# Where the combining of a band is traced: directly behind its deformable products instead of two slots later

## The chip, the cores and the metric

The kernel runs on one core of a Trainium2 chip. The metric is the device time of one execution in microseconds (us). Engines by the names of the profile: PE (TensorE: matrix products and transposes; PEld is its weight load), DVE (VectorE), ACT (ScalarE), POOL (GpSimd), and SP (SyncE, which here only issues DMAs). Each engine works through its own list of instructions in order.

## The reference

Two layers on 32 images of 96 channels and 56 x 56 pixels, float32.

Layer 0 is an inverted bottleneck: 1x1 convolution to 576 channels, normalisation and SiLU; a 3x3 depthwise convolution, normalisation and SiLU; a squeeze-and-excite gate; a 1x1 convolution back to 96 channels; the input is added.

Layer 1 is the part that the change touches (`sampled` are nine bilinear samples per pixel at learned offsets):

```python
y = x * ca * sa                                   # channel and spatial attention, from spectra
aux = concat([y, coord, freq_e], 1)
offset = conv3x3(aux, off_w)                      # 18 channels: 9 taps x 2
gate = sigmoid(conv1x1(relu(conv3x3(aux, dg1_w)), dg2_w))
y_base = conv3x3(y, base_w)
sampled = grid_sample_taps(y, xx + off[:, :, 0], yy + off[:, :, 1])
y_def = einsum('bcthw,oct->bohw', sampled, def_w) + def_b
z = (1 - gate) * y_base + gate * y_def
zn = (z - mean(z)) / sqrt(var(z) + 1e-5) * bn_g + bn_b    # over all images
return relu(zn + x)
```

## The kernel before

**Tiling.** Layer 1 goes through each image in 7 bands of 8 rows (224 bands in all, index `n`), and each band in two halves (h = 0, 1) of 7 blocks each 4 pixels wide. In this text half-band number 2n+h is called "half 2n+h". The samples of a block are a matrix product: `weights` multiplies two loaded tables `wc` and `wr` into sampling weights (one DVE instruction per half, L709; "product k" is the one for half k), `sample_tiles` multiplies transposed image blocks by them (PE, L738) and ACT copies the samples into a tile `v` (L742). `pack` (L749, ACT) moves the last two taps of `v` into free partitions. `deform` (L757, PE) then multiplies `v` by the deformable weights into the PSUM bank `pd`; both halves of a band write into the same bank, and there is one such bank. `combine` reads `pd` and forms z with three DVE instructions (L796, L797, L798) and its statistics with a fourth (L799). `store` writes z to memory (L1060, issued by POOL). After the last band of an image, L1067 joins the statistics.

**What runs beside it.** `layers` interleaves three Python generators into one stream of traced instructions. Beside the bands of image b run layer 0 and the attention of image b+1 (`attend`: L329, L396, L420, L379 and small products; L373 on POOL) and the hidden part of layer 0 of image b+2 (`hidden`: L169 on PE, L173 on ACT, nine taps on DVE, L260 and L262). `pump` advances these by one "slot" and runs what has been put into `later` with a slot number. `find` does the offsets of band n+2: joint convolution (L615), copy of the offsets (L664), a maximum (L675), base convolution (L644).

**The order around the change.** In each half the loop does: `prepare` (table loads by SP, L702 and L703); `sample_tiles` for the first 3 blocks; three slots; then, once per half, the `ends` of the half before (`end_half`: `deform`, and, after h = 1, `join`, which calls `combine`); then `block_channels` (L720 on POOL, transposes L724 on PE) where due; then `weights` for the next half; then `sample_tiles` for the other 4 blocks with four slots, and `pack`. So the deformable products of band n's second half are traced inside half 2n+2, and the next instruction that `weights` traces there is product 2n+3.

Rows of the next image arrive in the padded tile `yp` by SP (L594) with an attention factor by POOL (L596), and DVE multiplies them (L602).

**Who sets the final order.** Tile's scheduler reorders the traced instructions of each engine by priority (trace order) and by its own estimate of when inputs are ready, and it sets the semaphores. SP is excluded (`manual_schedule`): its order is the traced one. One instruction is pinned by hand:

```python
def weights(nc, p, wc, wr):
    p["tc"].keep_in_program_order(nc.vector.tensor_tensor(wc, wc, wr, ALU.mult))
    return wc
```

`keep_in_program_order` adds an edge without a semaphore: the instruction stays behind the one that was traced just before it on the same engine. It says nothing of later ones, and nothing of two pinned instructions among themselves unless other edges join them.

Of the kernel before, what the change touches and what calls it, by code (L numbers as in the profile page):

```python
# [751 lines left out]
def deform(nc, p, pd, v, h):  # L752

    out = pd[:C, :BW].rearrange("c (q w) -> c q w", q=RB)[:, :, h * W // 2 : (h + 1) * W // 2]
    for k in range(KA):
        ks = slice(0, 128 if k else C)
        nc.tensor.matmul(out.rearrange("c q (t x) -> c t q x", x=TS), p["w"]["def"][ks, k],  # L757
                         v[ks, k].rearrange("c t s (r x) -> c t (s r) x", r=TS),
                         start=(k == 0), stop=(k == KA - 1))
# [33 lines left out]
def combine(nc, p, j, pd, yb, gate, st):  # L793

    z = p["q2"].tile([C, BW], FP, name="z")
    nc.vector.scalar_tensor_tensor(z, pd[:C, :BW], p["w"]["cv"]("def_b"), yb, ALU.add, ALU.subtract)  # L796
    nc.vector.scalar_tensor_tensor(z, gate, 1.0, z, ALU.add, ALU.mult)  # L797
    nc.vector.scalar_tensor_tensor(z, z, 0.5, yb, ALU.mult, ALU.add)  # L798
    nc.vector.bn_stats(st[:, j], z)  # L799
    return z  # L800
# [152 lines left out]
def layers(tc, a, dp, x1d, zd, stats, far):  # L953
# [8 lines left out]
    with ExitStack() as ctx:  # L962
# [26 lines left out]
        streams, later = [], []  # L989
        slot = 0  # L990
# [68 lines left out]
        def store(b, j, z):  # L1059
            nc.gpsimd.dma_start(zd[b][:, j * BW : (j + 1) * BW], z)  # L1060

        def join(n, pd, gate, st):
            b, j = bands[n]
            z = combine(nc, p, j, pd, ybs[n], gate, st)
            later.append((slot + 7, lambda: store(b, j, z)))
            if j == NBD - 1:
                nc.vector.bn_aggr(stats[:, b], st)  # L1067

        def end_half(n, h, v, gate, st):
            if h == 0:  # L1070
                pds[n] = p["pd"].tile([128, 512], FP, name="pd")
            deform(nc, p, pds[n], v, h)
            if h:
                pd = pds.pop(n)
                later.append((slot + 2, lambda: join(n, pd, gate, st)))

        ends, pds = [], {}

# [41 lines left out]
        for n, (b, j) in enumerate(bands):  # L1120
            if j == 0:
                st = p["st"].tile([C, NBD, 6], FP, name="st")
# [7 lines left out]
            for h in range(2):  # L1130
                v = p["vp"].tile([128, NTAP, NTH, 2, TP], FP, name="v")
                prepare(2 * n + h + READY + AHEAD)
                s = ready.pop(0)
                yt = yts.pop(0)
                for i, group in enumerate(GROUPS):
                    sample_tiles(nc, p, yt, s, v, group)
                    for _ in range(group[0][0], group[-1][1]):
                        next(more, None)
                        pump()
                    if i == 0:  # L1140
                        for end in ends:
                            end()
                        ends.clear()
                        if h == 1 and n + 1 < len(bands):
                            yts.append(block_channels(nc, p, yp, bands[n + 1][1], 0))
                        ready.extend(weights(nc, p, *ws) for ws in loads[:1])
                        del loads[:1]
                        if h == 0:
                            yts.append(block_channels(nc, p, yp, j, 1))
                pack(nc, v)  # L1150
                if h == 0:
                    if n % 2 == 0:
                        gates.extend(gates_of(nc, p, hids[n // 2]))
                    gate = gates.pop(0)
                ends.append(lambda n=n, h=h, v=v, gate=gate, st=st: end_half(n, h, v, gate, st))
# [360 lines left out]
```

## Time and profile before

| | us |
|---|---|
| median of 3 runs | 9004.03 (8993.15 to 9010.88) |
| profiled execution | 8993.57, its span 8991.8 |
| PE busy | 8180.0 (91%) |
| DVE busy | 7174.8 (80%) |
| ACT busy | 5380.8 (60%) |
| POOL busy | 2600.4 (29%) |
| mean granted clock of TensorE | 0.94 |
| of this: one steady stretch, 4000 to 5000 | PE 953.68, DVE 842.19, ACT 622.27, POOL 318.64 |

The bands take the span from about 430 to 8705; the last 290 us are the normalisation. An image takes some 263 us. Images come in two forms that alternate, because the streams beside the bands don't divide evenly into slots; so a place in the order is the same again two images later. How to read it: "A <- B" in a list of waits is idle time of the engine of A, ended by B, as total, times, longest. In a timeline, "x3" merges three instructions of a line, and a bracket holds the idle time before the first of them and what ended it. A matmul instruction of the program on float32 shows as two records, a transpose as one.

### The profile page before, as it was taken

Reading aid. Unit: us, or ns where it says so; the run is one execution under the profiler, and the core shown is the slowest. Engines: PE = TensorE matmul, PEld = TensorE weight load, DVE = VectorE, ACT = ScalarE, POOL = GpSimd, SP = SyncE. Lnnn points to the kernel's source line nnn. Section 1 sums busy time; section 2 is a strip of 40 time slices with the busy share of each in tenths; the row PEclk is TensorE's granted clock in tenths of the full one; section 3 lists DMA queues with packets and bytes.
Section 4 is the critical chain, followed back from the end, with each engine's and each line's share of the span. In section 5 each row is a group of like instructions: output and inputs, shape, how many; then the busy total and the mean of one; then the engine's idle time right before and its main releaser. Section 6 shows DMA issues by size and latency. Waiting matters only on the chain. (4 is left out here: it accounts for less than half of the span.)

```text
span 8991.8 us, 137403 instructions
## 1 busy us (share of the span) xinstructions
PE 8180.0 (91%) x52406; PEld 5185.1 (58%) x52406; DVE 7174.8 (80%) x6821; ACT 5380.8 (60%) x10486; POOL 2600.4 (29%) x2608
## 2 busy tenths in 40 slices
PE   5899999999999999999999999999999999999960
PEld 3456565666656656665666666566566656666640
DVE  7688888888888888888888888888888888887333
ACT  2356666666666666666666666666666666666553
POOL 0133233333323332332332333233333323332210
PEclk9889999999999999999999999999999999999985
DMA  2356666666666666666666666666666666666669
GB/s 80 109 144 167 164 167 164 164 155 155 169 167 167 169 163 150 159 164 167 169 167 160 153 159 166 168 167 168 164 151 162 166 166 168 168 165 146 130 189 417
DMA packets 1068756, 1486.47 MB, mean 165 GB/s; under 512 B 590190, under 2 KB 839838, under 8 KB 1055806
## 3 DMA queue, kind: packets, MB, share of 16 engines
q1 hardware_dynamic: 858995, 985.20, 46.7%
q10 hardware_dynamic: 153803, 329.80, 10.2%
q0 software_dynamic: 55296, 162.60, 6.7%
q8 instruction: 420, 6.88, 0.4%
q14 instruction: 242, 1.98, 0.1%
HBM read 1064.29 MB, written 412.65 MB: 164 GB/s over the span
## 5 line engine op out<-in xcount | busy, mean ns | idle before, releaser
L262 DVE SCALAR_TENSOR_TENSOR acch<-hp,w,acch 128x1512 f32<-128x1512 f32 (+1 forms) x2250 | 4348.3, 1933 | 38.3
L615 PE MATMUL mm<-yp,c_jointW 104*128 104x448 f32 x4032 | 1655.9, 562 | 1.0 <-DMA yp<-fqd 1.0
L720 POOL COPY ybl<-yp 96x448 f32<-96x448 f32 x896 | 1035.1, 1183 | 1541.2 <-PE mm L724 1541.0
L757 PE MATMUL pd<-v,c_def 128*96 128x224 f32 (+1 forms) x6272 | 1429.6, 375 | 53.8 <-DVE z L796 29.0
L757 PEld LDWEIGHTS pd<-v,c_def 128*96 128x96 f32 (+1 forms) x6272 | 1039.5, 173 | 349.1 <-issue 74.5
L615 PEld LDWEIGHTS mm<-yp,c_jointW 104*128 104x128 f32 x4032 | 768.0, 194 | 758.2 <-issue 724.7
L738 PE MATMUL mm<-wc,yt 64*96 64x144 f32 x12544 | 1086.6, 302 | 115.7 <-ACT yb L649 44.8
L738 PEld LDWEIGHTS mm<-wc,yt 64*96 64x96 f32 x12544 | 845.6, 165 | 430.2 <-issue 193.2
L173 ACT ACTIVATE hp<-mm,sh,inv 128x392 f32<-128x392 f32 (+2 forms) x1216 | 812.0, 672 | 461.9 <-PE mm L169 416.4
L169 PE MATMUL mm<-xt,w 96*128 96x392 f32 (+3 forms) x2688 | 1056.8, 527 | 34.4 <-DMA xt<-in_x 33.4
L742 ACT COPY v<-mm 96x288 f32<-96x288 f32 (+1 forms) x2688 | 1003.6, 442 | 126.9 <-PE mm L738 81.4
L329 PE MATMUL mm<-hq,w3s 128*96 128x392 f32 x2048 | 796.8, 536 | 99.2 <-DMA hq<-h2d 92.4
L709 DVE TENSOR_TENSOR wc<-wc,wr 128x1008 f32<-128x1008 f32 x448 | 562.7, 1256 | 365.8 <-DMA wr<-hd 338.6
L644 PE MATMUL mm<-yp,c_base0W 96*64 96x224 f32 x8064 | 827.3, 357 | 0.0
L668 POOL DMA_DIRECT2D od<-at x224 | 185.6, 829 | 2217.9 <-DVE at L664 1515.6
L749 ACT COPY v<-v 32x448 f32<-32x448 f32 x1344 | 755.2, 562 | 29.7
L644 PEld LDWEIGHTS mm<-yp,c_base0W 96*64 96x64 f32 x8064 | 554.0, 135 | 275.4 <-issue 61.5
L726 ACT COPY yt<-mm 128x384 f32<-128x384 f32 (+1 forms) x896 | 350.5, 439 | 544.3 <-PE mm L724 543.8
L635 ACT ACTIVATE hid<-mm,c_dg1b 50x448 f32<-50x448 f32 x224 | 140.6, 628 | 862.9 <-PE mm L615 853.6
L329 PEld LDWEIGHTS mm<-hq,w3s 128*96 128x96 f32 x2048 | 339.1, 174 | 453.1 <-issue 311.0
L222 ACT ACTIVATE acch<-acch,sh,inv 128x1568 f32<-128x1568 f32 x288 | 488.3, 1695 | 180.3 <-DVE acch L262 167.0
L476 POOL TENSOR_TENSOR o<-o,xc 96x392 f32<-96x392 f32 x256 | 374.3, 1462 | 738.9 <-ACT o L339 737.3
(194 smaller groups left out, 9146.8 us busy)
## 6 DMA issues: line engine op xcount, KB each, us to landing
h2d<-acch ACTq DMA_DIRECT2D x288, 784.0 KB
wc<-hd SPq DMA_DIRECT2D x896, 252.0 KB
wr<-hd SPq DMA_DIRECT2D x448, 504.0 KB
hq<-h2d SPq DMA_DIRECT2D x128, 980.0 KB
hq<-h2d SPq DMA_DIRECT2D x128, 784.0 KB
hq<-x1d SPq DMA_DIRECT2D x768, 98.0 KB
ht<-od SPq DMA_DIRECT2D x224, 252.0 KB
hd<-ho ACTq DMA_DIRECT2D x224, 252.0 KB
```

Source lines behind the costliest of these rows:

```text
L169: nc.tensor.matmul(pt[p0 : p0 + w1.shape[1], : rows * W], w1, xts[hf][:, r0 * W : (r0 + rows) * W], start=True, stop=True)
L173: nc.scalar.activation(h1[lo:hi, row0 : row0 + rows, 1 : 1 + W], pt[lo:hi, : rows * W].rearrange("p (h w) -> p h w", h=rows), AF.Silu, bia ...
L262: nc.vector.scalar_tensor_tensor(acc[:, lo:hi], win, wk, acc[:, lo:hi], ALU.mult, ALU.add)
L329: nc.tensor.matmul(pts[half][:C, :EW], w3s[:, ch], hq, start=(i == 0), stop=False)
L615: nc.tensor.matmul(view, weights[:, k], yp[:channels, r0 : r0 + RB, dx + PD - 1 : dx + PD - 1 + W], start=(k == 0), stop=(k == NTAP - 1))
L644: nc.tensor.matmul(pb[i * BC : (i + 1) * BC, : BW // 2].rearrange("p (h w) -> p h w", h=RB // 2), w["base"][:, k], yp[:C, r0 + i * RB // 2 ...
L709: p["tc"].keep_in_program_order(nc.vector.tensor_tensor(wc, wc, wr, ALU.mult))
L720: nc.gpsimd.tensor_copy(yb[:, :, s], blocks)
L738: nc.tensor.matmul(pt[k][:C, (t - lo) * KP : (t - lo + 1) * KP], yt[ps, t], s[ps, t * KP : (t + 1) * KP], start=True, stop=True)
L742: nc.scalar.copy(v[:C, :, lo:hi, k].rearrange("c k t p -> c t k p"), pt[k][:C, : (hi - lo) * KP].rearrange("c (t k p) -> c t k p", t=hi - ...
L749: nc.scalar.copy(v[C:, 1 + 2 * i : 3 + 2 * i], v[i * QC : (i + 1) * QC, KA:])
L757: nc.tensor.matmul(out.rearrange("c q (t x) -> c t q x", x=TS), p["w"]["def"][ks, k], v[ks, k].rearrange("c t s (r x) -> c t (s r) x", r=T ...
```

## The change

`combine` is traced inside `end_half`, directly behind the deformable products of h = 1, instead of by `pump` two slots later. That puts it ahead of `block_channels`, of `weights` and of the second `sample_tiles` of the half, where before it came in the middle of the latter's slots. `store` is still put into `later` for 7 slots after the combining, so it comes two slots earlier as well. Nothing else changes: the instructions, their shapes and the pools are the same.

```diff
@@ def end_half(n, h, v, gate, st)
             deform(nc, p, pds[n], v, h)
             if h:
                 pd = pds.pop(n)
-                later.append((slot + 2, lambda: join(n, pd, gate, st)))
+                join(n, pd, gate, st)
```

## Prediction

> **What bounds the kernel now.** I read the page first, then busy time by stretches, the waits by engine, and the timeline of two stretches. Engine row of the page:
>
> ```profile
> PE 8180.0 (91%) x52406; PEld 5185.1 (58%) x52406; DVE 7174.8 (80%) x6821; ACT 5380.8 (60%) x10486; POOL 2600.4 (29%) x2608
> ```
>
> Stretches (us; busy of each engine; granted clock; DMA share; GB/s), two of them short ones around a wait of TensorE:
>
> ```profile
> 4000.00:5000.00 1000.00, 953.68 (x6125) 604.43 (x6123) 842.19 (x758) 622.27 (x1219) 318.64 (x315) 0.96 0.66 165
> ...
> 3628.40:3635.25 6.85, 4.88 (x8) 2.33 (x9) 5.99 (x3) 3.27 (x5) 4.31 (x4) 0.50 1.07 296
> ```
>
> TensorE (PE) works 954 us of each 1000, VectorE (DVE) 842. So a delay on DVE costs only where it makes PE wait. PE's list of waits says which DVE work does that today:
>
> ```profile
> PE mm L329 <- DMA hq<-h2d: 92.4, 30, 4.1
> ...
> PE pd L757 <- DVE z L796: 29.0, 25, 3.0
> ...
> PE mm L738 <- DVE wc L709: 4.6, 1, 4.6
> ```
>
> The combining holds PE 25 times (29.0 us, and 20.4 us more on PE's weight loads): the one `pd` bank isn't free yet. The weights product L709 holds it once. That is the term to watch, because the change moves L709.
>
> **What the change moves.** Six lines of trace order, no instruction more or less. `weights` (L709) is pinned: it may not pass the DVE instruction traced just before it. Before, in the half-bands with h=0 that instruction is some convolution or reduction. After, it is the last of the combining, L799 (L1067 in the last band of an image). In the built order of the changed kernel all 223 products of odd number stand behind the previous band's L799; before, 2 did. And L709 of the following even half, pinned to an older instruction, is no longer held behind it: in 67 places the pair is swapped, product 2n+2 ahead of 2n+1, two bands per image in images 1 to 30 and seven in the last image. SP's queue keeps its order to the instruction; POOL's differs by one store per image (L1060 ahead of L668); on ACT 268 of 10647 instructions are out of the old order, on PE 1121 of 27771: mainly deform products (L757) set ahead of the sampling L738 that now waits.
>
> So the wait added is L738's, for a product that comes late. Queued behind L738 on PE is everything: PE takes its matmuls in order. Queued ahead of L709 on DVE are L796 to L799 and what is dealt between them.
>
> **(a) Fourth band of each image.** Half 175, DVE and then PE, timeline before (start, us, line, idle before in brackets):
>
> ```profile
> 3756.03 0.69 DVE L664 COPY at<-mm 18x224 f32<-18x224 f32 x2
> 3756.65 1.44 DVE L709 TENSOR_TENSOR wc<-wc,wr 128x1008 f32<-128x1008 f32 x1
> 3758.01 0.60 DVE L675 TENSOR_REDUCE top<-at 18x1 f32<-18x448 f32 x1
> 3758.54 7.42 DVE L262 SCALAR_TENSOR_TENSOR acch<-hp,w,acch 128x1568 f32<-128x1568 f32 x3
> 3765.99 0.68 DVE L796 SCALAR_TENSOR_TENSOR z<-pd,c_cvec,yb 96x448 f32<-96x448 f32 x1
> 3766.59 1.96 DVE L262 SCALAR_TENSOR_TENSOR acch<-hp,w,acch 128x1512 f32<-128x1512 f32 x1
> ...
> 3773.62 0.61 DVE L799 BATCH_NORM_STATS2 st<-z 96x6 f32<-96x448 f32 x1
> 3776.81 0.68 DVE L602 SCALAR_TENSOR_TENSOR yp<-yp,ca,sab 96x448 f32<-96x448 f32 x1 [2.58 <-DMA yp<-x1d]
> ```
>
> ```profile
> 3764.87 1.05 PE L396 MATMUL mm<-c_FU,hq 112*128 112x116 f32 x8
> 3765.84 0.98 PE L738 MATMUL mm<-wc,yt 64*96 64x144 f32 x12
> ```
>
> Product 175 is done at 3758.1 and PE wants it at 3765.84: 7.8 us of slack. In the changed order DVE does L664, L675, four L262, L796, product 176, L797, L262, L798, then L602, L799 and only then product 175. L602 is the point: it reads rows whose DMA landed at 3776.81, and that landing hangs on the GpSimd and SP queues (GpSimd busy from 3752.44 to 3768.8 before it issued the offsets; SP issued the rows at 3772.01, behind the read of those offsets), which the change leaves alone. So 3776.81 + 0.68 + 0.61 (L799) + 1.19 (product) = 3779.3. PE arrives at 3765.84 with six deform instructions put ahead (12 of the 14 records that took 2.81: 2.4 us), themselves held until L796 frees `pd` at 3756.72 + 0.60 + 7.42 + 1.96 + 0.68 = 3767.4. PE therefore loses 3779.3 - 3765.84 - 2.4 = 11.1 us. Images come in two alternating forms; in the other one (half 161) L602 started at 3515.41, the product ends at 3517.9, L738 was due at 3502.87 and only two deform instructions (0.8 us) stand ahead: 14.2. Mean 12.7 us per image.
>
> **(b) First band of each image** (behind the last band's combining). Half 169: product 170 waits for its load until 3652.12 as before and ends at 3653.8; then two L262 (4.2), L796, L797, L798 (1.9), L379 (0.9), L799 and L1067 (1.0), product 169 (1.2): 3663.0. PE was due at 3658.23, one deform instruction now stands ahead (0.4 in half of the cases): 4.7 lost. In the other form (half 155) L379 could start only at 3400.18, when its rows had landed; 0.92 + 0.62 + 0.34 + 1.19 more give 3403.3, against 3393.94 and 0.4: 8.9, less the 1.4 that PE waited for `pd` right behind it and no longer does: 7.5. Mean 6.1.
>
> **(c) The five other odd halves of an image.** In three the delay (6.4 to 7.6 us) is within the slack (10.5 to 14.1) or nearly so (4.9 of 6.4). In two, halves 173 and 177, the product ends 4.5 and 5.5 us after L738's old start, but 1.9 to 3.5 us of other matmuls now stand ahead, and PE arrives later after (b) and (a) while DVE does not. I take 0; bounds 0 and 4 us.
>
> **(d) Clock.** When PE waited 3.52 us for `hq` (to 3630.36), the clock stood at 0.50 from 3628.40 to 3635.25, and the next eight L329 records took 5.26 us; the eight before took 2.87. A wait of 1.98 us at 3705.44 drew 6.8 us of half clock too. Two new waits per image at 2.4 each: 4.8. [...]
>
> **(e) What goes.** With PE this much later, the hidden rows that it waits for today (92.4 us in 30 waits, 3.1 per image) have landed, and their half clock (2.4) goes too: -5.5. Between -1 (they slip along with PE) and -9 (bank waits for ACT, 44.8 and 43.6 us in all, go as well).
>
> **(f) At nothing.** The earlier store of z (POOL is busy 29%) and the later release of `wr`: half 177's load, issued at 3774.41, slips to 3779.3, but its product isn't due before some 3805. Freeing `pd` earlier: 49.4 us of PE's waits is the most it can return; (b) has counted its part, and (a) adds one such wait, so 0.
>
> **Sum.** 12.7 + 6.1 + 4.8 - 5.5 = 18.1 us per image; 30 images: 543. The last image, with seven swapped pairs and DVE only 30% busy: four halves (433 to 439) end 11.5, 10.9, 9.2 and 5.6 us late, less 1.5 each for deform work put ahead: about 31. In all 574. The profiled execution took 8993.6 us (span 8991.8), 10.5 below the median of 9004.03: 8993.6 + 574 = 9568, say 9565.
>
> **Rivals.**
> 1. *The slack holds, about 9050.* DVE idles 15%; if it runs so far ahead that combining and product are done in time, only (a)'s landing stays, at part of its price: 30 x 2 us. Against: the slack of 7.8 us is measured with DVE as it is, and in (a) DVE has to wait for a landing, not for itself. 6 in 100.
> 2. *Faster, about 8950.* The only mechanism is `pd`: combining at once frees it, and the 49.4 us go. It decides only if product 2n+1 isn't late by more than about 1.5 us per image; seven products per image would each have to keep their slack. 3 in 100.
> 3. *It feeds back, about 9900.* DVE stands in front of L796 while PE is late, the convolutions behind it (L260, L262) stop, and so do hidden rows and ACT; then (e) is 0, (c) 4 and each image loses another 3 to 5 us: 30 x 28 + 31 = 871, 9865. For it: DVE at 84%. Against: the period grows by 7%, which gives DVE 18 us more per image. 13 in 100.
>
> **Numbers.** Forecast 78 in 100: 30 x (half of (a)+(b)) = 280 with nothing else gives about 9275 at its low end; all bounds at their dear end, 30 x 26.6 + 31, gives 9820. The range 9250 to 9820 leaves out rival 1 and 2 and part of 3. A change under 0.2% (18 us) can't be told from none: faster 0.03, same 0.03, slower 0.94.
>
> **What would show it.** Right: PE's waits list L738 <- L709 with about 60 waits near 10 us, 450 to 650 us together; granted clock below 0.94 in the mean; the wait for `hq` short. Wrong: if that row stays under 100 us, (a) and (b) are wrong, most likely by L602's landing being earlier. If PE's waits for ACT or `hq` grow, rival 3.

## The result, and the profile after

The changed kernel takes 9729.35 us (median of 4 runs, 9706.02 to 9749.40) against 8999.76 for the kernel before (8993.15 to 9010.88): a ratio of 1.081 (95% interval 1.078 to 1.084). It is slower by some 730 us; 565 were forecast. The profiled execution took 9721.11 us, its span 9719.3, which is 727.5 longer than before. Engine row of the page after:

```profile
PE 8441.1 (87%) x52406; PEld 5350.3 (55%) x52406; DVE 7176.6 (74%) x6821; ACT 5415.7 (56%) x10486; POOL 2704.7 (28%) x2608
```

The counts are those of before, and DVE is as busy as before (7176.6 against 7174.8). PE's part of the span splits the loss in two: 261 us more busy time for the same matmuls, and 9719.3 - 8441.1 = 1278 us idle where 812 stood, so 466 us more idle. Waits of PE after:

```profile
PE mm L738 <- issue: 479.1, 91, 11.3
PE mm L329 <- DMA hq<-h2d: 87.8, 27, 5.4
...
PE pd L757 <- DVE z L796: 49.7, 17, 8.4
```

The first row is new. The profile calls its releaser "issue": the wait for the product sits on PE's sequencer, ahead of the matmul (in half 175 a semaphore wait of 9.97 us of PE's weight-load queue, which ends at 4043.6, where the product's first L738 starts). Taken half by half, the first L738 of the halves concerned starts 0.10 us after the end of its own product L709 (median), so the releaser is L709. The same holds for 29 waits that the list puts under PE's own L757 (23.9 us) and 7 under ACT's L771 (34.3 us). Idle time of PE in front of such an L738 is 545 us in all, in 131 waits; 9.7 before. By half (halves 28 to 425, mean per image): first band's second half 4.9 us, third band's 0.9, fourth band's 9.3, fifth band's 2.0, the other three 0.

The fourth band of the image that was shown for before; DVE, then PE (start, length, line; idle before in brackets):

```profile
4030.26 0.68 DVE L796 SCALAR_TENSOR_TENSOR z<-pd,c_cvec,yb 96x448 f32<-96x448 f32 x1
4030.86 1.43 DVE L709 TENSOR_TENSOR wc<-wc,wr 128x1008 f32<-128x1008 f32 x1
...
4034.82 0.97 DVE L798 SCALAR_TENSOR_TENSOR z<-z,yb 96x448 f32<-96x448 f32 x1
4041.18 0.68 DVE L602 SCALAR_TENSOR_TENSOR yp<-yp,ca,sab 96x448 f32<-96x448 f32 x1 [5.39 <-DMA yp<-x1d]
4041.78 0.62 DVE L799 BATCH_NORM_STATS2 st<-z 96x6 f32<-96x448 f32 x1
4042.32 1.19 DVE L709 TENSOR_TENSOR wc<-wc,wr 128x1008 f32<-128x1008 f32 x1
```

```profile
4031.72 2.49 PE L757 MATMUL pd<-v,c_def 96*96 96x224 f32 x12
4043.61 1.85 PE L738 MATMUL mm<-wc,yt 64*96 64x144 f32 x12 [9.40 <-issue]
4045.39 1.67 PE L169 MATMUL mm<-xt,w 96*128 96x392 f32 x2
```

(This is half 175 again; it has moved from 3766 to 4044.) The first L709 is product 176, the second product 175: the pair is swapped, and product 175 stands behind the landing that L602 waits for. PE idles 9.40 us. Behind the wait the twelve L738 records take 1.85 us; before they took 0.98, at a granted clock of 1.00. Stretches around it (busy of PE, PEld, DVE, ACT, POOL; granted clock; DMA share; GB/s):

```profile
4034.00:4037.73 3.73, 0.21 (x2) 0.00 (x0) 1.78 (x2) 0.00 (x0) 2.67 (x3) 1.00 0.26 21
4037.73:4051.40 13.67, 7.79 (x39) 6.40 (x41) 6.44 (x7) 3.04 (x6) 1.68 (x4) 0.50 0.63 155
4051.40:4055.00 3.60, 3.60 (x34) 2.95 (x36) 3.56 (x2) 3.19 (x8) 1.97 (x1) 1.00 0.01 2
```

Half clock lasts 13.67 us, of which PE worked 7.79. Over the whole span, the long last stretch of the normalisation left out, PE works 1159 us at half clock, 685 before. The twelve L738 records take about twice their time at half clock (1.85 us against 0.98). If all of the work at half clock does, half of the 474 us difference, 237 us, is an estimate of what the clock adds: nearly all of the 261 us of busy time.

### The profile page after: what moved, and what is told of

It reads as the page before. It is cut to its first block, busy times and chain, and to the rows that moved or that the text cites. A ratio compares the mean times of both kernels' runs of the same rounds, so it can differ in the third digit from the quotient of the medians.

```text
span 9719.3 us, 137423 instructions
## 1 busy us (share of the span) xinstructions
PE 8441.1 (87%) x52406; PEld 5350.3 (55%) x52406; DVE 7176.6 (74%) x6821; ACT 5415.7 (56%) x10486; POOL 2704.7 (28%) x2608
## 3 DMA queue, kind: packets, MB, share of 16 engines
q1 hardware_dynamic: 858995, 985.20, 43.6%
## 5 line engine op out<-in xcount | busy, mean ns | idle before, releaser
L720 POOL COPY ybl<-yp 96x448 f32<-96x448 f32 x896 | 1152.9, 1314 | 2457.4 <-PE mm L724 2456.9
L615 PE MATMUL mm<-yp,c_jointW 104*128 104x448 f32 x4032 | 1702.2, 574 | 1.0 <-DMA yp<-fqd 1.0
L738 PE MATMUL mm<-wc,yt 64*96 64x144 f32 x12544 | 1179.3, 316 | 549.6 <-issue 479.1
L757 PE MATMUL pd<-v,c_def 128*96 128x224 f32 (+1 forms) x6272 | 1462.7, 381 | 96.4 <-DVE z L796 49.7
L738 PEld LDWEIGHTS mm<-wc,yt 64*96 64x96 f32 x12544 | 912.5, 174 | 853.6 <-issue 692.6
L757 PEld LDWEIGHTS pd<-v,c_def 128*96 128x96 f32 (+1 forms) x6272 | 1055.9, 176 | 419.0 <-issue 103.6
L615 PEld LDWEIGHTS mm<-yp,c_jointW 104*128 104x128 f32 x4032 | 788.9, 199 | 782.4 <-issue 747.1
L169 PE MATMUL mm<-xt,w 96*128 96x392 f32 (+3 forms) x2688 | 1118.6, 551 | 34.7 <-DMA xt<-in_x 33.6
L329 PE MATMUL mm<-hq,w3s 128*96 128x392 f32 x2048 | 774.6, 524 | 101.7 <-DMA hq<-h2d 87.8
L709 DVE TENSOR_TENSOR wc<-wc,wr 128x1008 f32<-128x1008 f32 x448 | 554.0, 1237 | 348.7 <-DMA wr<-hd 338.5
L260 DVE TENSOR_SCALAR acch<-hp,w 128x1568 f32<-128x1568 f32 x270 | 282.6, 1047 | 469.1 <-ACT hp L173 452.4
```

Source lines behind the costliest of these rows:

```text
L169: nc.tensor.matmul(pt[p0 : p0 + w1.shape[1], : rows * W], w1, xts[hf][:, r0 * W : (r0 + rows) * W], start=True, stop=True)
L329: nc.tensor.matmul(pts[half][:C, :EW], w3s[:, ch], hq, start=(i == 0), stop=False)
L615: nc.tensor.matmul(view, weights[:, k], yp[:channels, r0 : r0 + RB, dx + PD - 1 : dx + PD - 1 + W], start=(k == 0), stop=(k == NTAP - 1))
L720: nc.gpsimd.tensor_copy(yb[:, :, s], blocks)
L738: nc.tensor.matmul(pt[k][:C, (t - lo) * KP : (t - lo + 1) * KP], yt[ps, t], s[ps, t * KP : (t + 1) * KP], start=True, stop=True)
```

## The experiments

Theory: the time goes where a product (L709) that is pinned behind the combining holds PE's sampling, and into the half clock behind those waits. Rival: the early combining itself is dear, because it holds VectorE up in front of L796. Each kernel was compared with the kernel before on the same chip; the first four shared one set of its runs (median 9007.3), the next four another (9009.5), the last two a third (8995.8). In the diffs the changed kernel is the old side unless it is said otherwise.

### 1. The product traced first

```diff
                     if i == 0:
+                        ready.extend(weights(nc, p, *ws) for ws in loads[:1])
+                        del loads[:1]
                         for end in ends:
                             end()
 ...
-                        ready.extend(weights(nc, p, *ws) for ws in loads[:1])
-                        del loads[:1]
```

> The changed kernel, but weights is traced ahead of the ends, so the product of an odd half is pinned to the same instruction as before the change and not behind the combining; the combining stays directly behind its deformable products. Theory (the late product is the whole cost): about 9000 us, waits of TensorE at L738 near 0, granted clock 0.94; perhaps 8950 if freeing the pd bank sooner is worth its 49 us. Rival (the early combining itself costs, by holding VectorE in front of L796 while TensorE is late): 9400 or more, with VectorE's waits at L796 near the 448 us of the changed kernel.

9019.98 us, ratio 1.0015 (1.0003 to 1.0026). The combining is still directly behind its products, but 2 of 223 odd products stand behind it instead of all. Waits of DVE for `pd` and of PE for DVE's release of it in this kernel, and after them DVE's row of the changed kernel:

```profile
DVE z L796 <- PE pd L757: 215.3, 93, 12.0
...
PE pd L757 <- DVE z L796: 56.4, 30, 6.2
```

```profile
DVE acch L260 <- ACT hp L173: 452.4, 102, 10.6
DVE z L796 <- PE pd L757: 447.9, 96, 11.8
```

The rival falls: with the combining as early as in the changed kernel, DVE waits 215 us for `pd` (188 before), not 448, and the loss is gone. DVE's long waits in the changed kernel belong to the late product, not to the early combining. The gain from freeing `pd` earlier, up to 49 us, didn't come either: PE waits 56 us for it.

### 2. The pin taken away

```diff
-    p["tc"].keep_in_program_order(nc.vector.tensor_tensor(wc, wc, wr, ALU.mult))
+    nc.vector.tensor_tensor(wc, wc, wr, ALU.mult)
```

> The changed kernel with the pin on L709 taken away, nothing else. Theory: the scheduler puts the products ahead of the combining again, the cost of the change goes, and what is left is the worth of the pin itself: 9000 to 9150 us. Rival (early combining costs): stays above 9400.

9254.77 us, ratio 1.028 (1.026 to 1.030): two thirds of the loss go, and the expected upper end, 9150, is passed. PE's waits for products are down to 11.6 us. What is left comes with another order: products now float ahead to where their tables haven't landed, and DVE stands before them.

```profile
DVE wc L709 <- DMA wr<-hd: 706.7, 213, 15.6
```

It was 338.6 us in 120 waits before. Some of that reaches PE: its waits for DVE's small product L563 are 81.1 us, 4.4 before. That this is all of the 247 us that are left is not shown. With the combining traced early the pin is worth having (9020 us in number 1, 9255 without it); what counts is the instruction it is tied to.

### 3. One slot instead of two

```diff
 # against the kernel before
-                later.append((slot + 2, lambda: join(n, pd, gate, st)))
+                later.append((slot + 1, lambda: join(n, pd, gate, st)))
```

> The kernel before with the combining one slot after its deformable products instead of two; weights is still traced ahead of it. Theory: within 0.3% of the kernel before (8975 to 9025), since no product is pinned behind the combining. Rival (a dose of early combining costs a dose of time): about half of the change's loss, 9350.

8902.56 us, ratio 0.988 (0.986 to 0.990): faster than both kernels, which neither theory expected. There is no dose of loss in an earlier combining. The gain is PE busy time (8100.0 us against 8180.0) with the idle time as before (817 against 812). In the kernel before, PE waits twice per image for PSUM banks that ACT still reads, in the stretch behind half 176:

```profile
PE mm L738 <- ACT yb L649: 44.8, 29, 1.9
PE mm L738 <- ACT hp L173: 43.6, 31, 1.9
```

With one slot the first row is gone and the second is

```profile
PE mm L738 <- ACT hp L173: 5.8, 11, 1.7
```

and the half clock in their place, 10.0 us per image, is 0.4 (table below). That the waits draw this half clock is argued from the place; no run takes the waits alone away. The idle time itself came back at other places (L724 on POOL's copies, 37.2 us; L615 on the frequency rows, 34.4 us).

### 4. L602 kept out of the product's way

```diff
-    nc.vector.scalar_tensor_tensor(rows, rows, p["ca", b], sab, ALU.mult, ALU.mult)
+    p["tc"].keep_in_program_order(nc.vector.scalar_tensor_tensor(rows, rows, p["ca", b], sab, ALU.mult, ALU.mult))
```

> The changed kernel with L602 pinned behind the instruction traced before it, which takes it out from between L798 and L799 in the fourth band of an image. Theory (a): product 175 no longer waits for the landing of the rows and ends about 5.4 us sooner, so the wait of 9.3 us per image there falls to about 4, 160 us less in all and up to 60 us of clock: 9500 to 9600 us. Rival (the place of L602 is of no account, the product is late by VectorE's own work): 9700 to 9740.

9495.82 us, ratio 1.055 (1.051 to 1.058): just below the expected range, and some 235 us less than the changed kernel, by the medians as by the ratios. The wait in the fourth band is 4.8 us instead of 9.3, waits for products are 389 us in all instead of 545. In profiled executions 9719.3 - 9477.0 = 242 us less, 75 of them busy time of PE (8365.9). The landing of the rows was half of the wait in (a).

### 5 to 7. The change in some bands alone

```diff
-                join(n, pd, gate, st)
+                if bands[n][1] == 2:              # 6: == NBD - 1;  7: not in (2, NBD - 1)
+                    join(n, pd, gate, st)
+                else:
+                    later.append((slot + 2, lambda: join(n, pd, gate, st)))
```

> Of the change, only the combining of the third band of each image is traced directly behind its deformable products (so the late product is that of the fourth band's second half, step (a)); the six others keep their two slots. Theory: 31 waits of about 9.3 us and 3 to 4 us of half clock behind each, 9350 to 9500 us. Rival (the 9.3 us there are a consequence of what other bands do): under 9200.

> Only the combining of the last band of each image is traced directly behind its products (step (b)). Theory: 31 waits of about 4.9 us and 2 to 3 us of clock each, 9180 to 9320 us. Rival: under 9100.

> The change in all bands but the third and the last of each image (step (c), taken as 0 because TensorE would be late already). If the three parts add up, this is what the two others leave of the 727 us: 50 to 150 us, 9050 to 9150. If the parts of (c) were only covered by the lateness from (a) and (b), it is more: two waits of 2 us and their clock in each image, 9150 to 9260. If (c) is 0 by itself: 8990 to 9040.

| kernel | us | ratio to before (95%) | span over before | PE busy over before | PE idle over before | waits for products |
|---|---|---|---|---|---|---|
| changed, all bands | 9729.35 | 1.081 (1.078-1.084) | +727.5 | +261.1 | +466.4 | 545 |
| 5: third band alone | 9255.52 | 1.028 (1.025-1.032) | +244.6 | -22.7 | +267.3 | 308 |
| 6: last band alone | 9203.11 | 1.022 (1.020-1.025) | +212.2 | +80.9 | +131.3 | 161 |
| 7: the five others | 9236.43 | 1.026 (1.021-1.031) | +210.8 | +147.5 | +63.3 | 82 |

(Spans, busy and idle from each profiled execution, against 8991.8, 8180.0 and 811.8. Numbers 5 to 7 have two executions each; the two of number 7 are 64 us apart, and the profiled one is the shorter.) The first row of PE's waits for products in numbers 5, 6 and 7:

```profile
PE mm L738 <- issue: 300.2, 33, 11.2
```

```profile
PE mm L738 <- issue: 125.7, 26, 8.6
```

```profile
PE mm L738 <- issue: 49.8, 25, 4.6
```

The three spans add up to 668 of 727.5, so the parts are nearly independent, and each costs about as much as the others. But they pay in different coin. The long waits of number 5 cost idle time and no busy time in the sum. Number 7, with short waits of 0.9 and 1.1 us per image in the third and fifth band, has 147 us more busy time. That is neither what step (c) nor what step (d) of the prediction said, and number 5 stayed below its expected range, which had added a clock cost to each wait. Number 6 lies in its range. Number 7 lies in its second range, but not for the reason given there: its waits, 2.0 us per image, aren't longer than the 2.9 of the changed kernel, so the lateness from (a) and (b) had covered nothing.

Where the half clock lies, worked out from the clock's record: us of half clock per image, mean over 28 images, by the half-band (counted from 0 within the image) in which it began:

| half | before | changed | 5 | 6 | 7 | one slot (3) |
|---|---|---|---|---|---|---|
| 0 | 0 | 10.7 | 0 | 10.1 | 0 | 0 |
| 1 | 2.4 | 0.1 | 3.2 | 0.5 | 2.7 | 3.5 |
| 3 | 3.7 | 3.9 | 3.2 | 3.9 | 4.0 | 4.4 |
| 5 | 0.2 | 6.3 | 0 | 0.1 | 10.2 | 0.4 |
| 6 | 0 | 12.9 | 13.4 | 0 | 0 | 0 |
| 8 | 10.0 | 3.2 | 0 | 10.4 | 5.7 | 0.4 |
| others | 5.5 | 6.4 | 5.9 | 5.2 | 4.8 | 6.7 |
| sum | 21.8 | 43.5 | 25.7 | 30.1 | 27.4 | 15.4 |

Number 5 trades the 10.0 us of half 8 for 13.4 in half 6. Of these 13.4 PE is idle for 6.4, with no matmul to slow down; of the 10.0 before it was idle for 1.5. Number 6 adds 10.1 in half 0 and keeps most of the rest. Number 7 adds 10.2 in half 5, as 15 stretches of some 20 us in 28 images.

### 8. The combining last in its step

```diff
-                join(n, pd, gate, st)
+                joins.append(lambda: join(n, pd, gate, st))
 ...
                         if h == 0:
                             yts.append(block_channels(nc, p, yp, j, 1))
+                        while joins:
+                            joins.pop(0)()
 ...
```

> The combining traced in the same step as its deformable products, but behind block_channels and weights. Theory: no product is pinned behind it, so none of the change's loss: 8900 to 9020, between the kernel with one slot (8903) and the one with weights first (9020). Rival (any combining ahead of the next slot costs): over 9100.

9006.31 us, ratio 0.9998 (0.9985 to 1.0011), as expected. Together with number 1 it brackets the cause. In both the combining is early, and `weights` is traced ahead of it, so no product is tied to it; both take the time of the kernel before. The changed kernel, with `weights` behind the combining in the same step of the loop, takes 8% more.

### 9 and 10. Three slots, and the best kernel with L602 pinned

```diff
 # 9, against the kernel before
-                later.append((slot + 2, lambda: join(n, pd, gate, st)))
+                later.append((slot + 3, lambda: join(n, pd, gate, st)))
 # 10: the diff of 3 and that of 4 together
```

> The kernel before with the combining three slots after its deformable products instead of two. Theory of a slack that is wide on this side too (no product is pinned behind it, the pd bank is wanted again only in the next half): 8990 to 9060 us. If the gain of one slot (-1.2%) is a trend, the mirror of it: about 9100.

> One slot instead of two, and L602 pinned as in the run before that pinned it. If the rows' landing holds VectorE up in the best kernel too, some 20 to 60 us less than its 8903; if its gain of one slot is a matter of the clock alone, 8880 to 8960.

Number 9: 8931.39 us, 0.993 (0.992 to 0.995), below both of its expectations. Number 10: 8959.88, 0.996 (0.995 to 0.997). So one slot isn't a step of a trend: three are faster than two as well, with the same thing missing (half 8 has 0.2 us of half clock, 10.0 with two slots). Two slots happen to give an order in which PE runs into ACT's banks there. Why the scheduler deals it so, was not tried. Pinning L602 doesn't help the best kernel (57 us slower by medians, 68 by the ratios), though it helped the changed one: there it stood in front of a late product, here it doesn't. The fastest kernel of the case is number 3, 8902.56 us.

## Why the prediction was right, and where it was off

The mechanism held: the built order ties each odd product to the combining, PE idles in front of L738 until it comes, and the granted clock is at a half for longer (43.5 us per image, 21.8 before). Number 1 shows that this is all of the loss. Numbers 5 and 6 find two thirds of it, 457 of 668 us, in the two places that were priced; the last third, number 7, lies where step (c) put nothing. The excess in the span is 727.5 us, 574 were forecast. The sum came as near as it did partly because errors cancelled.

- **(a)**, 12.7 us per image forecast, 9.3 measured as wait for the product. That L602's landing sets the end was right, and in number 4 half the wait goes with L602. What failed is the distance between landing and PE. Read off the kernel before, L602 starts 11.0 us (half 175) and 12.5 us (half 161) behind PE's arrival; it is 9.5 in both halves of the changed kernel. So the wait for `pd` ahead of the deform instructions didn't occur in half 175 (9.4 lost, 11.1 forecast), and half 161 lost 10.9 instead of 14.2. In four of the fourteen images of the latter form DVE waits 1.5 us or less for the rows, and PE 3.6 to 4.9 for the product.
- **(b)**, 6.1 forecast, 4.9 measured. Half 169: 4.7 forecast, 5.0 measured. Half 155: 7.5 forecast, 3.0 measured as wait for the product. L379's rows, which were to hold DVE up there, had landed, and the wait for `pd` that was to go stayed:

```profile
3621.39 1.03 PE L757 MATMUL pd<-v,c_def 96*96 96x224 f32 x2 [1.89 <-DVE z L796]
3625.45 1.85 PE L738 MATMUL mm<-wc,yt 64*96 64x144 f32 x12 [3.03 <-issue]
```

- **(c)**, 0 forecast with a bound of 4 us per image; 2.9 us of waits measured (0.9 and 2.0 in the two halves named, and nothing in the three others, as said). The argument that PE would be late enough already was wrong, and the price in number 7 alone, 211 us or 6.6 per image, is above the bound, because it is mostly busy time (147.5 us).
- (a) to (c) together: 18.8 forecast, 17.1 measured. That they are so near is luck: (a) was 3.4 too dear and (c) 2.9 too cheap. The idle time too came near by luck: 30 x 18.8 + 31, less the 93 us (30 x 3.1) of (e), is 502, and 466 came, but the waits that went are others than those of (e).
- **(d)**, the mis-sized term. 30 x 4.8 = 144 us of clock were forecast, less 30 x 2.4 = 72 that were to vanish with the wait for `hq`: 72 net. PE's busy time rose by 261; these 189 us more, less 36 of idle time, are the miss. The step took a price per wait from two waits of the kernel before and counted two new waits per image. The runs show half clock in new places (halves 0, 5 and 6 of the table) in stretches of very different length, and no fixed price: number 5 has the longest waits and pays no busy time, number 7 the shortest and pays the most. What sets the length stays open.
- **(e)**, -5.5 per image forecast. The wait that it names stayed: 87.8 us for `hq`, 92.4 before. What went instead are the waits for PSUM banks that ACT still reads, which the step had only at its dear end. After, against 43.6 and 44.8 us before:

```profile
PE mm L738 <- ACT hp L173: 1.5, 2, 0.8
...
PE mm L738 <- ACT yb L649: 0.9, 1, 0.9
```

  With them the half clock in half 8 fell from 10.0 to 3.2 us per image. So there was relief, from another wait than the one argued for. That the hidden rows slip along with PE fits DVE's waits for ACT's `hp` at L260, 452 us against 196 before, since `hp` comes from PE's L169; no run tests it.
- **(f)**: the earlier release of `pd` returned nothing, as forecast; PE's waits for it are 49.7 us, 29.0 before.
- **The signs.** The waits for products are 545 us together, within the 450 to 650 named, but in 131 waits and not about 60: the two priced places have 57 of 7.1 us in the mean (halves 28 to 425). The clock fell to 0.907; the wait for `hq` did not become short.
- **The rivals.** Number 1 and 2 fell. Rival 3 stands as near to the result as the forecast does: its 9865 is 136 us off, 9565 is 164. It was right that `hq` brings no relief, that (c) is near 4, and that DVE stands longer in front of L796 (188 to 448 us) and L260. But the 3 to 5 us more per image that it drew from this aren't in PE's idle time, which stayed below the forecast's; the miss is busy time. Its sum leaves them out as well: 27.6 us per image are reached with (e) at 0 and (c) at 4, and with them it would be some 9940 to 10000.

## What to carry to other kernels

An order pin ties an instruction to whatever was traced just before it, so moving a piece of tracing across a pinned instruction moves the pin; before such an edit, read which instructions the pinned one comes to stand behind, and what DMA landing stands among them. Price a late input by its slack in the trace (7.8 us in the fourth band here), count the delays that come ahead of it, then look for the clock separately: number 3 and the kernel before have the same idle time of TensorE within 5 us, and 80 us between their busy times. And a delay of the busiest engine doesn't by itself swallow an existing wait (that for `hq` is 87.8 us here, 92.4 before): ask for each wait what it hangs on.

## What the runs showed of the hardware

A granted clock of one half needs no long wait here. In the changed kernel the clock fell 2.6 us after a wait of 0.74 us, in a stretch of narrow matmuls (L541, L543, L550, L557, and L738 among them), and stayed down for 20.5 us in which the records show PE without a gap. PE's timeline there, and the stretch:

```profile
3990.75 0.45 PE L738 MATMUL mm<-wc,yt 64*96 64x144 f32 x2 [0.74 <-PE pd L757]
...
3992.67 0.26 PE L544 MATMUL acc<-thM,fe 29*56 29x56 f32 x2
...
3993.28 1.62 PE L169 MATMUL mm<-xt,w 96*128 96x392 f32 x2
```

```profile
3993.36:4013.80 20.44, 20.44 (x65) 11.20 (x65) 12.94 (x11) 10.55 (x23) 3.35 (x2) 0.50 0.52 96
```

PE is busy all of 20.44 us with 65 matmuls. The same part of the kernel before, with the instructions in a slightly different order, at full clock:

```profile
3733.00:3753.00 20.00, 19.08 (x104) 10.91 (x105) 17.90 (x17) 13.63 (x33) 4.25 (x5) 1.00 0.83 168
```

There 104 records fit into as much time, with idle gaps of 0.58 and 0.34 us and no half clock. In the changed kernel a single short wait stands ahead of the fall, and PE shows no idle time in the 20.44 us of half clock that follow. The narrow shapes alone don't explain it, since they run at full clock in the kernel before. What keeps the clock down was not tested: no run changed the shapes alone.

The clock's records of these two profiled executions hold 112 stretches of half clock of 7.2 us in the mean before and 167 of 9.1 us after, the longest 34.1 and 30.7 us (the long last one, 286 and 287 us, aside). The shortest last 3.413 us (41 of them before, 49 after), and each of the others lasts a whole number of times that (the 13.67 us above four times, the 20.5 us six), to within 0.01 us. Their starts lie whole numbers of 3.4133 us apart too, to within 0.02 us. This is a reading of the two records; no run shows where it comes from. A stretch of half clock isn't in proportion to the wait at it: 20.5 us behind a wait of 0.74 us, 13.67 us from within the 9.40 us of half 175, 6.85 us from within the 3.52 us for `hq` in the kernel before.
